# A four-layer graph network: inverse roots on another engine, and every engine's instructions in the order of the program

## The chip, the core and the metric

The kernel runs on one core of one Trainium2 chip. A core has TensorE (PE in the profile: matrix products, with the weight loads shown apart as PEld), VectorE (DVE), ScalarE (ACT: functions from tables, which a table load switches), GpSimd (POOL), and SyncE (SP), which issues the DMA transfers here. Each engine has its own list of instructions, fixed when the program is built, and takes them one after the other; an instruction that needs another engine's result waits on a semaphore, and all behind it in that list wait with it. The metric is the device time of one execution in microseconds.

## The reference

64 graphs of 256 nodes with 128 features and an adjacency of zeros and ones (`x` is 64x256x128, `adj` 64x256x256, float32) go through four layers. After each layer the input is added and the sum normalised over the features:

- layer 0: `max_j relu(p_i + q_j + b) * adj_ij`, with `p = x (W1 - W2)` and `q = x W2`
- layer 1: `tanh([adj @ elu(x Win), elu(x Wnode), adjT @ elu(x Wout)] Wupd)`
- layer 2: two graph convolutions with `dinv_i (adj + I)_ij dinv_j`, where `dinv = 1/sqrt(degree)`, with elu between
- layer 3: for each edge `gelu(layernorm(m_j + m_i + b))` (128 features), summed over the neighbours; then a linear update with a layer normalisation of its own.

```
def _layernorm(x, axis=-1, eps=1e-5):
    m = jnp.mean(x, axis=axis, keepdims=True)
    v = jnp.var(x, axis=axis, keepdims=True)
    return (x - m) / jnp.sqrt(v + eps)
...
msg = jax.nn.gelu(_layernorm(pre, g1, be1), approximate=False)
agg = jnp.einsum('bijo,bij->bio', msg, adjacency)
```

## The kernel before

About one in eight entries of `adj` is set, so layers 0 and 3 work on edges, not on all pairs. For each graph the nodes are sorted by their number of neighbours, and the k-th neighbours of all nodes stand side by side in slot k of a row of 4800 columns for each half of the nodes. A one-hot matrix `hot` (fp8) picks the neighbour of each column. A product of `hot` with the features, which are split into three bf16 parts so that no precision is lost, fetches them: three matmuls for each 512 columns. If a graph didn't fit the slots, a flag would start a second way (`general`); with these inputs it is not run.

Each graph goes through four generators, in this order:

- `first` (L502 to L711): `nz` and `diff` from `adj` (L509, L511), the transposed adjacency `aT` (L516, L519), counts by matmul, the rank of each node by four ACT sign instructions (L551), the permutation `perm` (L560), the slots (`nzp`, `rank`, `lack`, L566 to L592), 24 DVE instructions that make `hot` (L629; the last slots L635), `q` split into three parts (L647 to L652), and ten tiles for each half: PE fetches 512 columns into one of four PSUM banks `bigp` (L665, and L681, which lowers empty slots), DVE takes the maximum into `lanes` (L492 in `fold`). Then come the way back through the permutation (L691 to L706), `y` (L709), and a layer normalisation.
- `second` (L215): layer 1, small products and elus (ACT exp, L194).
- `third` (L261 and L789 on): layer 2, the factors of layer 3 (L797 to L815), and the sums for the first four of the ten tiles of 1024 or 704 columns.
- `last` (L821): the rest of layer 3. For a tile, `sums_of` has PE fetch (L728), DVE add the node's own part (L732), ACT square (L736), PE sum the squares (L743) and ACT write a row (L745) that goes to DRAM; for two tiles together the row comes back as 16 columns (`vr`), is turned into `1/sqrt` (L768) and goes out again (L771); each tile's scale is spread to all partitions by a DMA (`rs_s`, L828). Then DVE multiplies (L839), ACT takes the gelu (L841), DVE adds up (L492, `sums`), and PE applies the output weights (L860) and the permutation (L870).

`inverse_root` (L72) is a Sqrt on ACT and a reciprocal on DVE. It is used by the layer normalisation on two columns (`rs`), for `dinv` on two, and for `vr` on 16.

`together` (L341) runs the four generators of four consecutive graphs next to each other: round u has `last` of graph u, `third` of u+1, `second` of u+2, `first` of u+3, and each is advanced by one `yield` at a time, in proportion to the weights in `STAGES` (L879). That is the order in which the program is written down. The order on each engine is another one: the recording layer has a scheduler that plans with its own estimate of durations, and places each instruction where it may start by that plan, so work of one round can pass work of the round before. Four PSUM banks `mm` (L357) go round among all stages for the small products. The load of `x` and `adj` stands at the start of `first`.

## Time and profile before

| what | us |
|---|---|
| time of the runs: median, lowest, highest of three | 5728.43, 5723.99, 5739.29 |
| the profiled execution: its own time | 5731.62 |
| its span in the profile | 5729.7 |
| PE busy (79% of the span) | 4529.9 |
| PEld busy (44%) | 2508.7 |
| DVE busy (84%) | 4834.4 |
| ACT busy (75%) | 4275.2 |
| POOL busy | 1.9 |
| mean granted TensorE clock, as a share of full speed | 0.862 |

A group's row in the profile has the line, the engine, the operation, output and input with their shapes and the number of instructions; behind the first bar their busy time and the mean length of one in ns; behind the second the idle time of the engine just before them, with what ended most of it. The chain of waits is followed back from the last instruction: at each step to what released it, or to the instruction before it on its engine. In the timeline a row has its start, its length, the engine and line, and what it is.

### The profile page before, as it was taken

To read this page: it belongs to the slowest core of one execution; us is meant where nothing else is said; L and a number is where in the kernel's file an instruction comes from. 1 tells how busy PE (TensorE), PEld (TensorE's weight loads), DVE (VectorE), ACT (ScalarE), POOL (GpSimd) and SP (SyncE) were. 2 spreads that over 40 slices of the span, in tenths; PEclk is the share of its full clock that TensorE was granted. 3 is DMA by queue.
4 is the path that set the end of the run, shared out by engine and by line. 5 is a ranking of instruction groups with operands and counts; after the bars stand their busy time and mean duration, and the time that the engine had idled before them with its cause. 6 is when DMAs were issued, how large, how long until landed. Compare 5 with 4: busy or idle time off the path is not lost.

```text
span 5729.7 us, 83531 instructions
## 1 busy us (share of the span) xinstructions
PE 4529.9 (79%) x27408; PEld 2508.7 (44%) x27408; DVE 4834.4 (84%) x14654; ACT 4275.2 (75%) x6485; POOL 1.9 (0%) x10
## 2 busy tenths in 40 slices
PE   5878878878778778788788788787887887877875
PEld 2444444444444444444444444444444444444443
DVE  6788888888888888888888888888888888888876
ACT  2577777777777777777777777777777777777785
POOL 0000000000000000000000000000000000000000
PEclk8888889889889889888898898898888887888986
DMA  0122222222212221221221222122212212221222
GB/s 22 44 70 63 62 63 72 62 63 66 69 57 70 65 63 63 72 63 62 63 72 62 63 65 70 59 68 65 63 62 72 64 62 63 69 66 60 68 65 74
DMA packets 292813, 365.15 MB, mean 64 GB/s; under 512 B 151952, under 2 KB 210448, under 8 KB 292368
## 3 DMA queue, kind: packets, MB, share of 16 engines
q1 hardware_dynamic: 292368, 359.73, 20.0%
q8 instruction: 217, 3.56, 0.3%
q14 instruction: 228, 1.87, 0.1%
HBM read 345.07 MB, written 14.53 MB: 63 GB/s over the span
## 4 chain that ended last, share of the span: by engine, by line
PE 52%; DVE 29%; ACT 11%; issue 4%; DMA 3%; SPq 0%; DVEq 0%; POOL 0%; ACTq 0%
PE bigp L665 11%; PE bigp L728 8%; DVE pre L839 6%; PE mm L860 5%; DVE lanes L492 4%; PE mm L743 4%; DVE hot L629 4%; DVE pre L732 4%; DVE sums L492 3%; PE bigp L681 3%; DMA rs_s<-scale_line 2%; PE mm L870 2%; PE mm L296 2%; PE mm L699 2%; PE mm L647 2%
## 5 line engine op out<-in xcount | busy, mean ns | idle before, releaser
L665 PE MATMUL bigp<-hot,q 128*128 128x512 fp8e4 (+1 forms) x3840 | 1052.3, 371 | 66.6 <-DVE lanes L492 52.6
L728 PE MATMUL bigp<-hot,c 128*128 128x512 fp8e4 (+1 forms) x3840 | 928.8, 372 | 140.2 <-DVE pre L732 140.2
L732 DVE TENSOR_TENSOR pre<-bigp,dT 128x512 f32<-128x512 f32 (+6 forms) x1664 | 846.3, 530 | 37.8 <-PE bigp L728 33.5
L492 DVE TENSOR_TENSOR lanes<-bigp,lanes 128x512 f32<-128x512 f32 (+6 forms) x1536 | 772.7, 503 | 94.6 <-PE bigp L681 86.9
L839 DVE TENSOR_TENSOR pre<-pre,rs_s 128x1024 f32<-128x1024 f32 (+1 forms) x640 | 732.9, 1150 | 48.6 <-DMA rs_s<-scale_line 48.0
L736 ACT ACTIVATE sq<-pre 128x1024 f32<-128x1024 f32 (+1 forms) x640 | 638.5, 998 | 169.9 <-DVE pre L732 163.9
L841 ACT ACT_TABLE_LOAD x535 | 686.4, 1283 | 9.5
L492 DVE TENSOR_TENSOR sums<-pre,sums 128x1024 f32<-128x1024 f32 (+6 forms) x1024 | 628.8, 614 | 41.2 <-ACT pre L841 40.7
L745 ACT ACTIVATE row<-mm,eps_t 128x256 f32<-128x256 f32 (+1 forms) x640 | 289.6, 453 | 476.9 <-PE mm L743 476.7
L841 ACT ACTIVATE pre<-pre,be,g 128x1024 f32<-128x1024 f32 (+1 forms) x512 | 594.2, 1172 | 57.8 <-DVE pre L839 53.0
L743 PE MATMUL mm<-sq,ones 128*32 128x256 f32 (+1 forms) x5120 | 482.9, 440 | 135.2 <-ACT sq L736 135.2
L74 ACT ACT_TABLE_LOAD x445 | 570.9, 1283 | 7.5
L728 PEld LDWEIGHTS <-c 128*128 128x128 bf16 x3840 | 331.2, 98 | 550.5 <-issue 136.1
L665 PEld LDWEIGHTS <-q 128*128 128x128 bf16 x3840 | 310.8, 97 | 392.6 <-issue 112.0
L296 PE MATMUL mm<-aT,hs 128*128 128x256 f32 x512 | 232.3, 600 | 316.1 <-DVE hs L293 214.8
L629 DVE TENSOR_SCALAR hot<-rank 128x512 fp8e4<-128x512 bf16 (+5 forms) x1536 | 440.5, 348 | 0.0
L681 PEld LDWEIGHTS <-pick 42*128 42x128 bf16 x2944 | 155.8, 95 | 481.5 <-issue 474.2
L296 PEld LDWEIGHTS mm<-aT,hs 128*128 128x128 f32 x512 | 135.6, 293 | 425.8 <-issue 316.1
L860 PE MATMUL mm<-w3u,sums 128*128 128x128 f32 x2048 | 296.7, 289 | 18.4 <-DVE sums L492 16.1
L194 ACT ACT_TABLE_LOAD x221 | 283.5, 1283 | 3.9
L681 PE MATMUL bigp<-lack,pick 42*128 42x36 bf16 (+16 forms) x2944 | 285.7, 187 | 0.0
L860 PEld LDWEIGHTS mm<-w3u,sums 128*128 128x128 f32 x2048 | 254.5, 195 | 37.3 <-issue 17.6
(226 smaller groups left out, 7132.6 us busy)
## 6 DMA issues: line engine op xcount, KB each, us to landing
rs_s<-scale_line SPq DMA_DIRECT2D x512, 512.0 KB
rs_s<-scale_line SPq DMA_DIRECT2D x128, 352.0 KB
an<-in_adj SPq DMA_DIRECT2D x64, 256.0 KB
x<-in_x SPq DMA_DIRECT2D x64, 128.0 KB
line<-row SPq DMA_DIRECT2D x512, 4.0 KB
out<-o SPq DMA_DIRECT2D x64, 128.0 KB
fu<-fulls SPq DMA_DIRECT2D x192, 4.0 KB
vr<-line SPq DMA_DIRECT2D x192, 8.0 KB
```

The lines of the kernel that those rows point to most:

```text
L74: nc.scalar.activation(t, t, AF.Sqrt)
L492: nc.vector.tensor_tensor(lanes[:, :k, :w], src[:, i:i + k], lanes[:, :k, :w], op)
L629: nc.vector.tensor_scalar(hot[:, :, at:at + w], rank[:, :, :w], s0 + i + 1.0 - FAR, None, ALU.is_equal, saturate=False)
L665: nc.tensor.matmul(pt[:, :tl], q3[:, i, h], hot[:, h, t0:t0 + tl], start=i == 0, stop=False)
L681: nc.tensor.matmul(o_, l_, r_, start=False, stop=i == len(todo) - 1)
L728: nc.tensor.matmul(pt[:, :bl], c3[:, k, h], hot[:, h, t0 + b:t0 + b + bl], start=k == 0, stop=k == 2)
L732: nc.vector.tensor_add(block(pre[:, b:], n, w, at), block(pt, n, w, at), widen(dT[:, h, :w], n))
L736: nc.scalar.activation(sq[:, :tl], pre[:, :tl], AF.Square)
L743: nc.tensor.matmul(pr[q * Q:(q + 1) * Q, :tl // 4], ones[:, :Q], v4[:, :, q], start=True, stop=True)
L839: nc.vector.tensor_mul(pre[:, :tl], pre[:, :tl], rs[:, :tl])
L841: nc.scalar.activation(msg[:, :tl], pre[:, :tl], AF.Gelu, bias=be3, scale=g3)
L860: nc.tensor.matmul(pt[:, cols], lanes[:, k, cols], w3u[:, 1], start=k == 0, stop=False)
```

## The change

- `inverse_root` becomes one GpSimd instruction, the power with exponent -0.5 (a tile `mhalf`). The two products that follow it, for `vr` and `dinv`, go to GpSimd as well.
- The whole edge-wise path is recorded with `tc.manual_schedule` for all five engines: each takes its instructions in the order in which the program writes them.
- The generators are cut into more steps: a `yield` stands wherever the work passes from one engine to another, so that steps of other graphs come between. The weights in `STAGES` are new.
- Each stage has one PSUM bank `mm` of its own (tags `_f`, `_s`, `_t`, `_l`) in place of four shared by all, and small tiles of its own. The four `bigp` banks stay.
- `dinv` is worked out in `first`; in layer 2, `aT` is scaled by it once (two DVE instructions of 128x256) in place of `hs` twice (four of 128x128).
- `x` and `adj` of a graph are loaded at the end of `first` of the graph before. The transposes of `perm` move beside the making of `hot`. Each fetch of `first` stands one tile ahead of the maximum.
- Layer 3 runs five tiles ahead (was four), with `pre` in eight buffers (was seven); `row` has one buffer (was two), `rs_s` two (was three). The way of `vr` through DRAM is a generator of its own (`scales`), advanced by one step with each step of its stage. The scale of a tile is fetched one tile ahead (was two).

```diff
-    half = consts.tile([P, N], F32, name="half")
-    nc.vector.memset(half, 0.5)
+    mhalf = consts.tile([P, 16], F32, name="mhalf")
+    nc.vector.memset(mhalf, -0.5)
     def inverse_root(t):
-        nc.scalar.activation(t, t, AF.Sqrt)
-        nc.vector.reciprocal(t, t)
+        nc.gpsimd.tensor_tensor(t, t, mhalf[:t.shape[0], :t.free_size()], ALU.pow)
...
             nc.vector.tensor_scalar(rs, mv[:, :, 1], EPS, None, ALU.add)
-            yield
             inverse_root(rs)
+            yield
             yield
...
             if twice:
                 nc.vector.tensor_scalar(e, e, 1.0, None, ALU.min)
+                yield
                 nc.scalar.activation(e, e, AF.Exp, bias=minus1)
...
+        def inverse_root_of(self, deg, bufs):
+            nc.vector.tensor_scalar(deg, deg, 1.0, None, ALU.add)
+            pos = self.work.tile([P, H], F32, name="pos" + self.tag)
+            nc.vector.tensor_scalar(pos, deg, 0.0, None, ALU.is_gt)
+            dinv = self.state.tile([P, H], F32, name="dinv", bufs=bufs)
+            nc.vector.tensor_scalar(dinv, deg, 1e-30, None, ALU.max)
+            inverse_root(dinv)
+            nc.gpsimd.tensor_mul(dinv, dinv, pos)
+            return dinv
...
+            for h in range(H):
+                nc.vector.tensor_scalar(aT[:, h], aT[:, h], dinv[:, h:h + 1], None, ALU.mult)
...
             for step in (1, 2):
-                for h in range(H):
-                    nc.vector.tensor_scalar(hs[:, h], hs[:, h], dinv[:, h:h + 1], None, ALU.mult)
...
-        ps_mm = ctx.enter_context(tc.tile_pool(name="ps_mm", bufs=4, space=bass.MemoryType.PSUM))
+        ps_mm = ctx.enter_context(tc.tile_pool(name="ps_mm", bufs=1, space=bass.MemoryType.PSUM))
...
-        sh = Shared(work, state, ps_mm)
-        psum = sh.psum
+        sh_f, sh_s, sh_t, sh_l = (Shared(work, state, ps_mm, tag) for tag in ("_f", "_s", "_t", "_l"))
...
+        def loads(g, s):
+            s["x0"] = xn = sh_f.node_tile("x0")
+            nc.sync.dma_start(xn, x[ds(g, 1)].rearrange("b (h p) d -> p (b h) d", p=P))
+            s["an"] = an = state.tile([P, H, N], F32, name="an")
+            nc.sync.dma_start(an, adj[ds(g, 1)].rearrange("b (h p) j -> p (b h) j", p=P))
...
+            nc.vector.tensor_scalar(dg, dg, 1.0 / N, None, ALU.mult)
+            s["dinv"] = sh_f.inverse_root_of(dg, 4)
+            yield
...
                         sign, pd[:, h * N:(h + 1) * N], AF.Sign, bias=kc[:, hi, h:h + 1], accum_out=more[:, h, hi:hi + 1]
                     )
             yield
+            yield
...
+            pts = {0: fetch_tile(*banks[0])}
+            yield
...
+            for k, (h, t0, tl) in enumerate(banks):
+                if k + 1 < len(banks):
+                    pts[k + 1] = fetch_tile(*banks[k + 1])
+                pt = pts.pop(k)
+                next(rest, None)
+                if t0 == 0:
+                    lanes = work.tile([P, 2, N], F32, name="lanes")
+                    nc.scalar.copy(lanes, pt.rearrange("p (s k) -> p s k", s=2))
+                else:
+                    fold(lanes, pt, t0, tl, ALU.max)
+                if t0 + tl == WIDTH:
+                    rest = largest(h, lanes)
+                    next(rest)
+                yield
...
+            if "next" in s:
+                loads(*s["next"])
+            s["x1"] = sh_f.node_tile("x1")
+            yield from sh_f.layernorm(s["x1"], y)
...
-        AHEAD = 4
+        AHEAD = 5
...
+        def scales(s, i, line):
+            yield
...
+            nc.sync.dma_start(vr[:rows], line[:, :n].rearrange("o (p k) -> (o p) k", k=PIECE))
...
+            yield
             inverse_root(vr[:rows])
-            nc.vector.tensor_mul(vr[:rows], vr[:rows], fu[:rows])
+            nc.gpsimd.tensor_mul(vr[:rows], vr[:rows], fu[:rows])
+            yield
...
+        def with_chains(s, gen):
+            for _ in gen:
+                for c in list(s["chains"]):
+                    if next(c, s) is s:
+                        s["chains"].remove(c)
+                yield
...
             for i in range(len(TODO) + 1):
+                square_sums(s, i + AHEAD - 1, psum)
+                gather_tile(s, i + AHEAD)
                 if i < len(TODO):
+                    spread_scales(s, i + 1)
...
                     nc.vector.tensor_mul(pre[:, :tl], pre[:, :tl], rs[:, :tl])
                     msgs[i] = msg = pre if t0 else big.tile([P, TILE], F32, name="sums")
                     nc.scalar.activation(msg[:, :tl], pre[:, :tl], AF.Gelu, bias=be3, scale=g3)
                     yield
+                if i + AHEAD - 1 < len(TODO):
+                    squares_out(s, i + AHEAD - 1)
+                    add_own(s, i + AHEAD)
+                    yield
...
-        STAGES = [(last, 34), (third, 34), (second, 14), (first, 44)]
+        IN_ORDER = ("PE", "Activation", "DVE", "Pool", "SP")
+        STAGES = [(last, 35), (third, 42), (second, 18), (first, 58)]
...
+        with tc.manual_schedule(engines={mybir.EngineType[e] for e in IN_ORDER}):
+            if U == B:
+                steps(0)
```

`sums_of` is cut into `gather_tile` (PE), `add_own` (DVE, then the square on ACT), `square_sums` (PE) and `squares_out` (ACT and the DMA); `spread_scales` is the DMA of `rs_s`.

## The prediction

> **What bounds the kernel now.** I read the busy totals first, then the busy times of one round, then the start times of one graph's `first`, and the groups of instructions and the waits last.
>
> ```profile
> PE 4529.9 (79%) x27408; PEld 2508.7 (44%) x27408; DVE 4834.4 (84%) x14654; ACT 4275.2 (75%) x6485; POOL 1.9 (0%) x10
> ...
> PE 52%; DVE 29%; ACT 11%; issue 4%; DMA 3%; SPq 0%; DVEq 0%; POOL 0%; ACTq 0%
> ...
> L841 ACT ACT_TABLE_LOAD x535 | 686.4, 1283 | 9.5
> ...
> L74 ACT ACT_TABLE_LOAD x445 | 570.9, 1283 | 7.5
> ...
> L194 ACT ACT_TABLE_LOAD x221 | 283.5, 1283 | 3.9
> ```
>
> No engine is full, and the chain of waits changes engine all the time. 1236 table loads (x 1.283 = 1586 us) are over a third of ACT's time. Next, one round from the view of busy times by stretch (length; PE, weight loads, DVE, ACT and POOL busy; PE's granted clock; DMA share; GB/s), and then from the view by source line when a line's first and last instruction in some rounds start.
>
> ```profile
> 2007.40:2094.70 87.30, 71.40 (x440) 39.54 (x439) 74.86 (x229) 66.51 (x104) 0.00 (x0) 0.90 0.20 65
> ```
>
> ```profile
> L509 DVE TENSOR_SCALAR nz<-an x3: 422/422/423, 2008.2 to 2182.4; 128x512 bf16<-128x512 f32 x3
> ...
> L665 PE MATMUL bigp<-hot,q x60: 246/379/634, 2071.9 to 2115.3; 128*128 128x512 fp8e4 x54, 128*128 128x192 fp8e4 x6
> ...
> L709 DVE SCALAR_TENSOR_TENSOR y<-m,x x2: 415/417/419, 2036.8 to 2123.9; 128x256 f32<-128x256 f32 x2
> ```
>
> `nz`, the first step of `first`, comes every 87.1 us (2008.2, 2182.4 two rounds later). PE is busy for 71.4 of that, DVE for 74.9, ACT for 66.5. The graph whose `nz` is at 2008.2 fetches its tiles (L665) from 2071.9 to 2115.3, and has its `y` (L709) at 2123.9: its `first` takes 116 us, 29 us more than a round. It fits because the `nz` of the next graph is at 2096.2, 28 us before that `y`. This overlap of two `first` stages is what I look at most.
>
> **Prices.** They are the rows by shape; the timeline shows that neighbours on one engine overlap (the add at 2094.57 lasts 0.69 and the next begins after 0.60), so in sums I take start to next start, and the full length where another engine waits.
>
> ```profile
> L839 DVE TENSOR_TENSOR pre<-pre,rs_s 128x1024 f32<-128x1024 f32 x512 | 622.3, 1216 | 22.8 <-DMA rs_s<-scale_line 22.2
> ...
> L736 ACT ACTIVATE sq<-pre 128x1024 f32<-128x1024 f32 x512 | 538.7, 1052 | 167.2 <-DVE pre L732 163.9 <-DVE total_m L688 3.1 <-DVE hs L308 0.2
> ...
> L841 ACT ACTIVATE pre<-pre,be,g 128x1024 f32<-128x1024 f32 x384 | 476.6, 1241 | 55.8 <-DVE pre L839 51.8
> ...
> L551 ACT ACTIVATE sign<-mm,kc 128x256 bf16<-128x256 f32 x256 | 121.1, 473 | 5.6 <-DVE dg L544 2.5 <-DVE kc L542 1.9
> ```
>
> ```profile
> 2094.57 0.69 DVE L732 TENSOR_TENSOR pre<-bigp,dT 128x512 f32<-128x512 f32 x1
> 2095.17 0.68 DVE L492 TENSOR_TENSOR lanes<-bigp,lanes 128x512 f32<-128x512 f32 x1
> ...
> 2038.85 1.28 ACT L74 ACT_TABLE_LOAD   x1
> 2040.14 0.20 ACT L74 ACTIVATE rs<-rs 128x2 f32<-128x2 f32 x1
> ```
>
> **The root on POOL.** Gone from ACT: 576 square roots (64.4 + 40.5 + 27.6 + 13.0 = 145 us) and, with the new order, 731 table loads: the built order has 505 where there were 1236. At 1.283 us, with no gap before the next instruction (2038.85 + 1.28, then 2040.14), that is 938 us; ACT falls to some 3190 us, 50 us a round. From DVE go the reciprocals (137 us), two small products (59 us) and L293 (61 us); scaling `aT` adds 128 at about 0.3 (39 us). Added up from start to start, 73.3 us a round are left of 75.2. Neither saving shortens a round unless ACT or DVE ended it.
> [...]
> POOL gets 17 instructions a round (1088 in all). The trace has no such power. From below I take its shortest row, 0.10 us; from above its longest, 0.45 (the select of 42x192), although a power may exceed it: its powers have 2 columns (six) or 16 (five), nearest to the small rows. A power takes the place of a load, a root and a reciprocal (1.28 + 0.20 + 0.15), and most have a step of cover on DVE: I take 0. At 2 us each, two or three would stand bare at the ends of `layernorm`, +5 us a round.
> [...]
>
> **The order.** Now all of `first` of a graph comes before all of `first` of the next in every engine's list: the 28 us of overlap are gone, and a round can't be shorter than one `first` with everything that the lists put between its steps. I added up the lists of one full round, with 0 at the start of `nz`.
> *To the split of q.* Before it DVE has 36.2 us: five multiplies L839 5.4, adds L732 5.9, sums L492 4.8, one-hot L629 and L635 7.0, the rest 13.1. At six places it has nothing left that it may do:
> - `kc`: the `aT` copy stands behind a square, which stands behind adds ending at 3.4; square to 4.5, copy 4.8, transpose 5.1, copy 5.5, counts 5.9. DVE is at 4.5: 1.4 us.
> - adds: their gather (PE square sums 0.70, three matmuls 0.69) follows the counts, so 7.3 instead of 6.7: 0.6. They end at 8.7.
> - `place`: that square to 9.8, four signs at 0.56 to 12.1, or 12.4 if the matmuls of `pd` (10.0) come late; DVE is done at 9.4: 3.0.
> - the first elu: load and exp (1.28 + 0.42) end at 14.1, DVE at 13.6: 0.5.
> - the second: the multiply ends at 16.3, then ACT has gelu 1.24, a copy 0.5, a load 1.28 and the exp 0.5, to 19.8. DVE has adds of 1.2: 2.4.
> - `lack_t`: the multiply ends at 22.8; load to 23.5, gelu to 24.7, `lack` 0.69, to 25.4: 2.6.
>
> Together 10.5, so the split is done at 46.7.
> *The fetch.* PE's list has the 2.6 us of L860 in front; 1.1 of it are late. From the first fetch to the end of the last it has 35.4 us (sixty L665 and their L681: 17.9; L728 4.1, L743 1.4, L860 2.6, L870 and L325 2.6, the layers' matmuls the rest). DVE's 25.8 beside it are hidden. PE can't be ahead: the four `bigp` banks and q hold it.
> *The tail.* DVE's remaining 11.3, with 1.8 of waits (0.6 for the last gather, 0.8 for `m0` behind sixteen L699, the rest for `mk`): 13.1. `x` and `adj` of the next graph are fetched in its cover: at the start of the trace `an` took 3.0 us from issue (32.6) to `nz` (35.6), and SP reaches the issue before the last 5 us. SP stops at each DMA that waits for ACT or POOL, but what stands behind it (`rs_s`) is used 8 us later: 0, at most 3.0 a round if `an` is late.
>
> Round: 46.7 + 1.1 + 35.4 + 13.1 = 96.3 us, against 87.2.
> **The sum.** There are 61 full rounds; 5729.7 - 61 x 87.2 = 410 us are the preparation and six partial rounds, which I leave, since less overlap there stands against less ACT work. 410 + 61 x 96.3 = 6284; the waits I could not see (semaphores, DMA) add a little: 6290. The profiled run took 5731.6 us, 1.9 more than its span and 3.2 more than the median of 5728.4, so nothing is corrected.
>
> **Rivals.** The round that changes nothing is 87.2, so 4.3 us of waits at the joints on top of 36.2 + 35.4 + 11.3 = 82.9 decide.
> 1. *The joints close* (faster): ACT's 938 us less were what held DVE, and the lists run without the waits above: 410 + 61 x 82.9 = 5467, up to 5711. For it: ACT is full (4.3 of 4.4 us) in most slices between `sign` and `hot` of the round shown, half with loads. Against it: the three largest waits (8.0) hold from row lengths alone. It decides where all waits are below 4.3 us.
> 2. *Half of the waits*: of the 13.4 us of waits (10.5 + 1.1 + 1.8) half stay: 82.9 + 6.7 = 89.6, 5876 us. For it: some of my PE prices are those of a low clock (L296 0.43 from start to start, where L238 of the same shape takes 0.23).
> [...]
> 4. The root doesn't leave ACT: the built order has no Sqrt, so I give it nothing.
>
> **Chances.** My forecast, 6080 to 6560 (rounds of 93 to 100.8): 0.57. Rival 2, 5780 to 6080 and down to +0.3%: 0.14. Rival 3, above 6560: 0.05. Within 0.3%, about what a measurement of this kernel can tell from no change: 0.03. Rival 1: 0.21. So slower 0.76, same 0.03, faster 0.21. The range from 5640 to 6560 holds the first two, the same and a quarter of rival 1: 0.79. The forecast's own range is 6080 to 6560.
>
> **What would show it.** Right: table loads 505; ACT below 3300 us; `nz` to `nz` near 96 with the next `nz` *after* `y`; DVE busy near 4690 us but 75% of the span; waits of DVE for `sign`, `lack` and the elu's exp of 2 to 3 us, 64 times each. Wrong: rounds below 87 with PE and DVE both above 80%; or POOL rows above 1 us with DVE waiting for `rs`. I am wrong if DVE reaches those places later than my sums say, so that ACT is ready.

## The result and the profile after

The changed kernel takes 6895.3 us (median; 6893.2 to 6895.3) where the kernel before takes 5728.4: **1.203 times as long, 95% interval 1.200 to 1.206**. The forecast of 6290 us had the direction and less than half of the loss; the time lies outside its range of 5640 to 6560.

The profiled execution took 6893.2 us with a span of 6891.4. Busy times, and one group of table loads, from its page:

```profile
PE 4900.1 (71%) x27408; PEld 2668.3 (39%) x27408; DVE 5027.4 (73%) x13438; ACT 3228.2 (47%) x5050; POOL 1570.9 (23%) x1098
...
L954 ACT ACT_TABLE_LOAD x252 | 323.3, 1283 | 4.4
```

ACT fell by 1047 us, as its loads did (1236 to 505). PE and DVE have the same or less to do and are *longer* busy: by 370 and 193 us. A round, from the view of busy times by stretch, and the steps of one `first`, from the view by source line:

```profile
3078.70:3184.50 105.80, 75.94 (x428) 41.46 (x428) 77.90 (x209) 50.63 (x79) 24.54 (x18) 0.82 0.18 53
```

```profile
L523 DVE TENSOR_SCALAR nz<-an x2: 417/418/419, 3078.7 to 3184.7; 128x512 bf16<-128x512 f32 x2
...
L698 PE MATMUL bigp<-hot,q x60: 246/379/634, 3130.8 to 3167.0; 128*128 128x512 fp8e4 x54, 128*128 128x192 fp8e4 x6
...
L765 DVE SCALAR_TENSOR_TENSOR y_f<-m,x x1: 426/426/426, 3180.6 to 3180.6; 128x256 f32<-128x256 f32 x1
```

A round is 105.8 us (before 87.2, forecast 96.3), and the next `nz` comes 4.1 us after `y`: the two `first` no longer overlap. The fetch starts 52.1 us after `nz`, takes 36.2 from its first start to its last, and 17.7 are left behind that. Two rows of the timeline stand ahead of the fetch, the end of the split of `q` (3127.77, 49.1 us after `nz`) and L938 (L860 before), ahead of which PE stood for 4.80 us:

```profile
3127.34 0.43 DVE L510 TENSOR_TENSOR q<-rest,q 128x256 bf16<-128x256 f32 x1
3126.12 2.04 PE L938 MATMUL mm_l<-w3u,sums 128*128 128x128 f32 x8 [4.80 <-DVE sums L501]
```

The groups of DVE and ACT that the sum was made with have kept their lengths:

```profile
L952 DVE TENSOR_TENSOR pre<-pre,rs_s 128x1024 f32<-128x1024 f32 x512 | 623.0, 1217 | 36.9 <-DMA rs_s<-scale_line 36.9
L803 ACT ACTIVATE sq<-pre 128x1024 f32<-128x1024 f32 x512 | 540.2, 1055 | 1136.1 <-DVE pre L799 1122.9 <-DVE y_s L272 4.4 <-DVE z L184 3.7
L954 ACT ACTIVATE pre<-pre,be,g 128x1024 f32<-128x1024 f32 x384 | 477.7, 1244 | 615.7 <-DVE pre L952 614.9
...
L569 ACT ACTIVATE sign<-mm_f,kc 128x256 bf16<-128x256 f32 x256 | 120.1, 469 | 12.7 <-PE mm_f L562 6.4
```

The waits (engine and tile that waited, what for; us in total, how often, the longest):

```profile
DVE lanes L501 <- PE bigp L714: 661.9, 458, 4.6
DVE place L575 <- ACT sign L569: 194.2, 64, 3.3
DVE m L762 <- ACT m L760: 162.0, 64, 5.0
DVE lack_t L618 <- ACT lack L604: 157.8, 64, 4.2
DVE elu_e_t L201 <- ACT elu_e_t L199: 150.8, 64, 2.4
DVE kc L552 <- PE mm_f L546: 93.0, 64, 2.2
```

Divided by 64: `place` 3.03 us, `lack_t` 2.47, the second elu 2.36, `kc` 1.45. The forecast had 3.0, 2.6, 2.4 and 1.4. But two rows are not as forecast: `m` (2.53 a round; 0.8 was taken) and DVE's wait for the fetch (662 us; 86.9 before). The rest of the document looks for the 9.5 us a round that were not foreseen.

### The profile page after: what moved, and what is told of

Read it like the earlier page. It is cut to its first block, busy times and chain, and to the rows that moved or that the text cites. A ratio compares the mean times of both kernels' runs of the same rounds, so it can differ in the third digit from the quotient of the medians.

```text
span 6891.4 us, 81950 instructions
## 1 busy us (share of the span) xinstructions
PE 4900.1 (71%) x27408; PEld 2668.3 (39%) x27408; DVE 5027.4 (73%) x13438; ACT 3228.2 (47%) x5050; POOL 1570.9 (23%) x1098
## 5 line engine op out<-in xcount | busy, mean ns | idle before, releaser
L75 POOL TENSOR_TENSOR vr<-vr,mhalf 128x16 f32<-128x16 f32 (+1 forms) x320 | 1195.6, 3736 | 1606.8 <-DMA vr<-line 1603.3
L698 PE MATMUL bigp<-hot,q 128*128 128x512 fp8e4 (+1 forms) x3840 | 1078.9, 392 | 7.2 <-ACT q L505 6.4
L786 PE MATMUL bigp<-hot,c 128*128 128x512 fp8e4 (+1 forms) x3840 | 1010.7, 406 | 0.0
L952 DVE TENSOR_TENSOR pre<-pre,rs_s 128x1024 f32<-128x1024 f32 (+1 forms) x640 | 735.9, 1150 | 37.6 <-DMA rs_s<-scale_line 37.6
L501 DVE TENSOR_TENSOR sums<-pre,sums 128x1024 f32<-128x1024 f32 (+6 forms) x1024 | 637.2, 622 | 17.7
L938 PE MATMUL mm_l<-w3u,sums 128*128 128x128 f32 x2048 | 406.6, 361 | 323.6 <-DVE sums L501 323.6
L75 POOL TENSOR_TENSOR rs_s<-rs_s,mhalf 128x2 f32<-128x2 f32 x64 | 44.5, 696 | 2237.3 <-DVE rs_s L174 2237.3
L938 PEld LDWEIGHTS mm_l<-w3u,sums 128*128 128x128 f32 x2048 | 358.2, 260 | 376.3 <-issue 347.0
L661 DVE TENSOR_SCALAR hot<-rank 128x512 fp8e4<-128x512 bf16 (+5 forms) x1536 | 458.6, 352 | 0.0
L698 PEld LDWEIGHTS <-q 128*128 128x128 bf16 x3840 | 323.1, 102 | 268.3 <-issue 45.3
L954 ACT ACTIVATE sums<-pre,be,g 128x1024 f32<-128x1024 f32 x128 | 158.7, 1240 | 496.0 <-DVE pre L952 496.0
L305 PE MATMUL mm_t<-aT,hs 128*128 128x256 f32 x512 | 253.5, 650 | 139.0 <-DVE hs L202 139.0
L814 PE MATMUL mm_l<-sq,ones 128*32 128x256 f32 (+1 forms) x3072 | 305.7, 481 | 32.1 <-ACT sq L803 32.1
L305 PEld LDWEIGHTS mm_t<-aT,hs 128*128 128x128 f32 x512 | 151.7, 326 | 451.6 <-DVE hs L202 428.8
L814 PE MATMUL mm_t<-sq,ones 128*32 128x256 f32 x2048 | 189.7, 447 | 162.9 <-ACT sq L803 162.9
```

Source lines behind the costliest of these rows:

```text
L75: nc.gpsimd.tensor_tensor(t, t, mhalf[:t.shape[0], :t.free_size()], ALU.pow)
L305: nc.tensor.matmul(pa[:, :N], hs[:, h], aT[:, h], start=h == 0, stop=h == H - 1)
L501: nc.vector.tensor_tensor(lanes[:, :k, :w], src[:, i:i + k], lanes[:, :k, :w], op)
L661: nc.vector.tensor_scalar(hot[:, :, at:at + w], rank[:, :, :w], s0 + i + 1.0 - FAR, None, ALU.is_equal, saturate=False)
L698: nc.tensor.matmul(pt[:, :tl], q3[:, i, h], hot[:, h, t0:t0 + tl], start=i == 0, stop=False)
L786: nc.tensor.matmul(pt[:, :bl], s["c3"][:, k, h], s["hot"][:, h, t0 + b:t0 + b + bl], start=k == 0, stop=k == 2)
```

## The experiments

Times are medians, ratios stand against the kernel before on the same chip, and "round" is `nz` to `nz` in the steady part of the trace (before 87.2, changed 105.8).

**The root by itself, the order by itself.** First the root alone is undone in the changed kernel.

```diff
-        nc.gpsimd.tensor_tensor(t, t, mhalf[:t.shape[0], :t.free_size()], ALU.pow)
+        nc.scalar.activation(t, t, AF.Sqrt)
+        nc.vector.reciprocal(t, t)
```

> The changed kernel with the root alone put back (Sqrt on ACT, reciprocal on DVE); lists, steps and PSUM banks as in the changed kernel. Theory 'order' (the slowdown comes from lists that follow the program): the root's place matters little to the end. A layernorm then ends on a load, a root and a reciprocal (1.28 + 0.20 + 0.15 = 1.63 us) where the power takes 0.70; the 16-column powers of 4 us become about 1.8 us, but most of these lie beside DVE work; up to 730 more loads come at joints where ACT is waited for: 6850 to 7250 us, never near 5728. Theory 'POOL' (the powers of 0.7 and 4 us, and POOL beside DVE, make the loss): a round loses most of its 19 us more, so 5730 to 6300 us, and L501, L799 and L952 become shorter or wait less.

Measured: 7667.9 us, ratio 1.340 [1.338, 1.342], 1212 table loads, a round of 117.9. In ordered lists the root on POOL does not cost, it saves 773 us, more than the expectation allowed: DVE waits 788.8 us for the root of `vr` alone.

Then the order alone is undone, everything else as changed.

```diff
-        with tc.manual_schedule(engines={mybir.EngineType[e] for e in IN_ORDER}):
-            if U == B:
...
+        if U == B:
```

> The changed kernel's program, buffers, banks and POOL root, but the engines' lists are made by the planner as before instead of following the program. Theory 'order': most of the loss goes, 5500 to 5900 us; nz of the next graph lies before y again or DVE's start-to-start times fall back (L501 at 0.62, L171 at 0.45). Theory 'banks': if a PSUM bank and single buffers for each stage forbid the overlap whatever the order, it stays above 6300 us with DVE and PE waiting for each other at the shared tiles. Theory 'POOL': above 6300 us with waits for the powers.

Measured: 5943.2 us, 1.040 [1.038, 1.043], 43 above what the theory of the order expected. **The fixed lists cost 952 us of the loss of 1167; what is left, 215 us, is the program.** Where those are, three kernels tell. Two are the kernel before, planned, with the power in place of the root: everywhere, and only for two columns.

```diff
-        nc.scalar.activation(t, t, AF.Sqrt)
-        nc.vector.reciprocal(t, t)
+        nc.gpsimd.tensor_tensor(t, t, mhalf[:t.shape[0], :t.free_size()], ALU.pow)
```

> The kernel before with the root alone moved to POOL; the planner orders the engines and 'first' of two graphs overlaps as before. Theory 'order': ACT loses some 700 loads and 576 roots (about 1000 us of 4370), POOL is waited for at few places because two graphs give the planner other work: 5450 to 5740 us, nz to nz 83 to 87.3 us. Theory 'POOL': powers of 0.7 and 4 us stand bare at the ends of the normalisations, or DVE becomes longer row by row: 5950 us or more. If ACT's loads were no bound at all, within 0.5% of 5728.

```diff
+        if t.free_size() == 2:
+            nc.gpsimd.tensor_tensor(t, t, mhalf[:t.shape[0]], ALU.pow)
+            return
         nc.scalar.activation(t, t, AF.Sqrt)
```

> The kernel before, planned, with the power on POOL only where the root has two columns (rs, dinv; 384 of them at 0.70 us by the run with all of them); the 16-column roots stay on ACT. Theory 'long powers' (the loss of 272 us in the run with all powers is DVE standing 752 us before the product with fu for powers of 2.9 us and more): that wait is gone, and ACT still loses some 390 roots and their loads: 5600 to 5740 us. Rival 'any power' (0.70 us bare at each end of a normalisation, or a planner that orders worse when ACT is lighter): 5800 to 6000 us.

Measured: 5997.8 us with all powers, 1.049 [1.047, 1.050], and 5688.9 us with the short ones, 0.994 [0.992, 0.996]. With all powers ACT is busy for 3096 us instead of 4275, with 379 table loads, and no gain is seen. The short powers alone make ACT 404 us lighter (954 loads), and the time falls by 0.6%. So ACT's load hardly bounded the kernel before. What the long powers cost is this wait, of DVE with the product that follows the power on `vr`:

```profile
DVE vr L770 <- POOL vr L76: 752.2, 319, 5.1
```

The third is the changed program, planned, with the 16-column roots back on ACT and DVE.

```diff
-        nc.gpsimd.tensor_tensor(t, t, mhalf[:t.shape[0], :t.free_size()], ALU.pow)
+        if t.free_size() == 2:
+            nc.gpsimd.tensor_tensor(t, t, mhalf[:t.shape[0], :2], ALU.pow)
+            return
+        nc.scalar.activation(t, t, AF.Sqrt)
+        nc.vector.reciprocal(t, t)
...
-        with tc.manual_schedule(engines={mybir.EngineType[e] for e in IN_ORDER}):
```

> The changed kernel's program, banks and single buffers, planned, with the 16-column roots back on ACT and DVE; the two-column ones stay on POOL. Theory 'long powers' (they alone cost the planned changed kernel its 220 us, as they cost the kernel before 309 us between all powers and short powers): 5600 to 5740 us. Rival 'banks' (a bank and buffers for each stage take freedom from the planner): 5800 us or more.

Measured: 5751.3 us, 1.005 [1.003, 1.006], 11 above the range for the long powers. 192 of the 215 us go with them; they lie on the way of the scale: DVE waited 565.5 us for `rs_s` with them, and 42.4 without. While the order is planned, a PSUM bank and buffers for each stage cost next to nothing (23 us are left); in fixed lists no run tells their price.

**Is it the lost overlap?** The forecast put the loss on the 28 us by which two `first` overlapped. In the kernel before, planned, an instruction was put behind `y` that reads `nz`, so that the only `nz` tile stays taken; first one that reads `nz` alone, then one that reads `y` too.

```diff
             nc.vector.scalar_tensor_tensor(y, m0, 0.0, xn, ALU.max, ALU.add)
+            held = work.tile([P, 1], BF16, name="held")
+            nc.vector.tensor_tensor(held, nz[:, 0, :1], y[:, 0, :1], ALU.max)
```

> The kernel before, planned as before, but nz is held until y: a DVE copy of one column of nz after y (128 elements, about 0.1 us) keeps the only nz tile, so nz of the next graph can't come before y. Leaves nothing else out. Theory 'order, by the overlap': the 28 us of overlap are gone while the planner still interleaves the other stages, so a round is one 'first' plus the turn from y to nz. 'first' was 116 us when it shared the engines with the next one; alone it may shrink. Theory expects nz to nz of 95 to 112 us, 6200 to 7250 us in all. Rival 'the overlap is worth little, the list itself (dependent neighbours, waits at the head) is what costs': nz to nz stays under 91 us, under 5960 us.

> The kernel before, planned, and nz held until y by a DVE instruction of one column that reads nz and y (the only nz tile can't be written again before it; in the run before this one the copy read nz alone, and the planner put it 10 us after nz, so it held nothing). Theory 'overlap' (the two 'first' stages beside each other are what the ordered lists lose): the next nz comes after y, a round becomes one 'first' of 95 to 116 us, 6200 to 7490 us. Rival 'lists' (the planner makes up for the overlap with the other stages; what costs in the changed kernel is the fixed order within a stage): a round stays under 91 us, 5700 to 5960 us.

The first was placed 18 us behind `nz` (not 10, as the second expectation says), far ahead of `y`, so it held nothing and changed nothing (5726.7 us, 1.0005 [0.9995, 1.0015]). The second did what it should, and **the time fell**: 5679.5 us, 0.993 [0.991, 0.994]. By source line, four rounds of it:

```profile
L509 DVE TENSOR_SCALAR nz<-an x4: 391/396/399, 2019.4 to 2278.6; 128x512 bf16<-128x512 f32 x4
...
L709 DVE SCALAR_TENSOR_TENSOR y<-m,x x4: 418/420/421, 2017.9 to 2277.1; 128x256 f32<-128x256 f32 x4
```

Each `nz` now comes 1.5 us after a `y`, and three rounds take 259.2 us, 86.4 each; a `first` alone takes 84.9 us instead of 115.4 on average. The overlap was slack that the planner had and did not need. The theory of the lost overlap falls, and with it the sentence that the forecast looked at most.

**Whose list is it?** The changed kernel with DVE's list alone planned, and with those of PE and ACT planned.

```diff
-        IN_ORDER = ("PE", "Activation", "DVE", "Pool", "SP")
+        IN_ORDER = ("PE", "Activation", "Pool", "SP")
```

> The changed kernel with DVE's list alone made by the planner; PE, ACT, POOL and SP keep the program's order. Theory 'DVE's list' (dependent neighbours on DVE, +322 us from start to start and 132 us of short gaps, and DVE standing at the head of its list for sign, lack, m and the elus, 760 us): DVE takes other work there and a good half of 1150 us comes back: 5750 to 6350 us, L501 and L171 at their old start-to-start times. Rival 'graph order' (PE's and ACT's lists alone forbid the overlap, and each engine's fixed list makes the others wait): 6600 to 7000 us.

```diff
-        IN_ORDER = ("PE", "Activation", "DVE", "Pool", "SP")
+        IN_ORDER = ("DVE", "Pool", "SP")
```

> The changed kernel with the lists of PE and ACT made by the planner; DVE, POOL and SP keep the program's order. With DVE's list alone planned 622 us of the 952 between the ordered and the planned changed kernel came back. Theory 'DVE's list' (it alone sets the round: it stands still in its places and its dependent neighbours cost): less than 150 us come back, 6750 to 6910 us. Rival 'shares add up' (PE's and ACT's fixed lists own the other third by themselves): 952 - 622 = 330 us come back, 6480 to 6650 us.

Measured: 6272.9 us (1.096 [1.094, 1.098], round 95.6) and 6247.1 us (1.092 [1.090, 1.094], round 95.3). Each gives back about two thirds of the 952 us, 622 and 648; for the second, one theory expected less than 150 and the other 330. The shares don't add up: no one list owns the loss. That it comes where two fixed lists meet, so that freeing either side of the meeting place gives most of it back, is argued from this, not shown place by place.

**Is it the length of the powers?** A POOL product by 0.001 in their place, which leaves the inverse roots out.

```diff
-    nc.vector.memset(mhalf, -0.5)
+    nc.vector.memset(mhalf, 1e-3)
...
-        nc.gpsimd.tensor_tensor(t, t, mhalf[:t.shape[0], :t.free_size()], ALU.pow)
+        nc.gpsimd.tensor_tensor(t, t, mhalf[:t.shape[0], :t.free_size()], ALU.mult)
```

> The changed kernel with a POOL product by 0.001 in place of each power (leaves the inverse roots out; the same tiles, lists and waits, rows of some 0.2 us instead of 0.70 and 2.9 to 4.1). The difference to the changed kernel is the price of the power's length in an ordered list. Theory 'order': six short powers of which up to five are bare, 0.5 us each, and the long ones in the cover of DVE's work: 2.5 us a round at most 4, 6640 to 6860 us. Theory 'POOL': the powers stand on the chain at every normalisation and sums line: 10 us a round or more, below 6300 us.

Measured: 6888.8 us, ratio 1.204 [1.202, 1.206], 7 us less. The rows of POOL in the changed kernel, and then in this one:

```profile
L75 POOL TENSOR_TENSOR vr<-vr,mhalf 128x16 f32<-128x16 f32 x192 | 779.7, 4061 | 1174.5 <-DMA vr<-line 1174.5
...
L75 POOL TENSOR_TENSOR rs_l<-rs_l,mhalf 128x2 f32<-128x2 f32 x128 | 89.1, 696 | 223.5 <-DVE rs_l L174 223.5
```

```profile
L75 POOL TENSOR_TENSOR vr<-vr,mhalf 128x16 f32<-128x16 f32 x192 | 277.6, 1446 | 1341.0 <-DMA vr<-line 1340.6 <-issue 0.2
...
L75 POOL TENSOR_TENSOR rs_l<-rs_l,mhalf 128x2 f32<-128x2 f32 x128 | 25.0, 195 | 453.4 <-DVE rs_l L174 453.4
```

2.6 us less for each long row and 0.5 for each short one, and almost nothing is won, less than either theory expected. No step of the round comes earlier: the fetch starts 52.3 us after `nz` and `y` 102.2 (52.0 and 101.8 with the powers). In these ordered lists the powers' length is covered, or nearly: by DVE's own waits it stood bare for 22.7 us (`rs_f`). A few tenths of a microsecond a round could be hidden here, since both rounds are 105.8 us for the reason found under "Whole windows".

**What lies next to what on DVE.** The planned kernel puts other work between instructions that feed each other; the program's order does not. From the timeline, the statistics of a normalisation before, and then after:

```profile
2036.84 0.42 DVE L709 SCALAR_TENSOR_TENSOR y<-m,x 128x256 f32<-128x256 f32 x1
2037.17 0.34 DVE L180 TENSOR_SCALAR o<-z,mv,rs 128x128 f32<-128x128 f32 x1
2037.43 0.48 DVE L171 BATCH_NORM_STATS2 st<-y 128x6 f32<-128x128 f32 x2
2037.82 0.17 DVE L172 BATCH_NORM_AGGREGATE mv<-st 128x2 f32<-128x6 f32 x1
```

```profile
3180.61 0.43 DVE L765 SCALAR_TENSOR_TENSOR y_f<-m,x 128x256 f32<-128x256 f32 x1
3181.07 0.29 DVE L171 BATCH_NORM_STATS2 st_f<-y_f 128x6 f32<-128x128 f32 x1
3181.40 0.18 DVE L172 BATCH_NORM_AGGREGATE mv_f<-st_f 128x2 f32<-128x6 f32 x1
3181.50 0.26 DVE L171 BATCH_NORM_STATS2 st_f<-y_f 128x6 f32<-128x128 f32 x1
3181.80 0.18 DVE L172 BATCH_NORM_AGGREGATE mv_f<-st_f 128x2 f32<-128x6 f32 x1
3182.01 0.17 DVE L174 TENSOR_SCALAR rs_f<-mv_f 128x2 f32<-128x2 f32 x1
```

Before, `o` begins 0.09 us before `y` ends. After, a `bn_aggr` begins 0.04 *behind* the end of the `bn_stats` that it reads. Over the whole trace of the changed kernel, a neighbour (at most 50 ns behind) that by its tiles' names reads or overwrites the tile just written begins 22 ns before its forerunner's end on average, another one 83 ns before it; and there are 7449 of the first kind to 4745 of the second (before: 4101 to 9223). The 22 ns is a mean of two values: 3612 of the 7449 begin 83 ns before the end as strangers do, many on another part of the same tile, and 3837 begin behind it, by 34 ns in the median (before: 457). Such a pair costs 117 ns more than two strangers. One experiment moves two such pairs in each normalisation apart.

```diff
             for h in range(H):
                 nc.vector.bn_stats(st[:, h], src[:, h])
+            for h in range(H):
                 nc.vector.bn_aggr(mv[:, h], st[:, h])
```

> The changed kernel, ordered, with one thing moved: in a normalisation the two bn_stats come first and then the two bn_aggr, so that no bn_aggr directly follows the bn_stats that it reads. Theory 'dependent neighbours' (in this kernel's DVE list a neighbour that reads its forerunner's output begins 22 ns before its end, another 83 ns): two joints of each of the five normalisations win about 0.06 us, 0.6 us a round, 40 us: 6840 to 6865 us. Rival 'they don't matter, DVE waits elsewhere anyway': within 0.2% of the changed kernel, 6881 to 6909 us.

Measured: 6692.1 us, 1.169 [1.167, 1.171]: 203 us less, five times the expectation. In its trace the statistics take 0.74 us from the first `bn_stats` to `rs`, where the rows above take 0.94:

```profile
3090.51 0.49 DVE L171 BATCH_NORM_STATS2 st_f<-y_f 128x6 f32<-128x128 f32 x2
3090.91 0.30 DVE L173 BATCH_NORM_AGGREGATE mv_f<-st_f 128x2 f32<-128x6 f32 x2
3091.25 0.17 DVE L175 TENSOR_SCALAR rs_f<-mv_f 128x2 f32<-128x2 f32 x1
```

Five times 0.20 is 1.0 us a round, 61 us; the round fell by 3.4, and the fetch starts no earlier (52.0 us after `nz`). Another thing must have moved.

**TensorE at half clock.** In the changed kernel's trace the clock that is granted to PE is 1.00 or 0.50, in 323 stretches of each, and each stretch but the last, which the end of the trace cuts off, takes a whole number of windows of 3.413 us (81 take one). PE's rows give it away. By shape, before, and then after:

```profile
L860 PE MATMUL mm<-w3u,sums 128*128 128x128 f32 x2048 | 296.7, 289 | 18.4 <-DVE sums L492 16.1
...
L699 PE MATMUL mm<-mk,permT 128*128 128x128 f32 x1024 | 127.7, 279 | 0.0
```

```profile
L938 PE MATMUL mm_l<-w3u,sums 128*128 128x128 f32 x2048 | 406.6, 361 | 323.6 <-DVE sums L501 323.6
...
L754 PE MATMUL mm_f<-mk,permT 128*128 128x128 f32 x1024 | 217.2, 401 | 0.9 <-ACT mk L729 0.9
```

These are the same matmuls under new line numbers. From one start to the next, L938 takes 112 ns at a clock of 1.00 and 213 at 0.50 in the median, and so does L754. And by stretch, one window of the clock, and then the two places in one round of the changed kernel, ahead of the fetch and ahead of `m` (the third number from the end is the granted clock):

```profile
3120.77:3124.18 3.41, 0.56 (x3) 0.15 (x1) 3.24 (x14) 2.90 (x4) 0.10 (x1) 1.00 0.46 150
3126.10:3130.80 4.70, 4.68 (x21) 3.86 (x22) 3.21 (x8) 1.29 (x2) 2.89 (x1) 0.50 0.38 114
3175.90:3179.30 3.40, 3.40 (x22) 3.28 (x24) 1.34 (x6) 0.80 (x2) 0.00 (x0) 0.57 0.66 222
```

PE stood 4.80 us before the first place (its wait for `sums`) and 1.30 and 1.97 us, with little work between, before the second. Added up over the trace, 1071 us of PE's busy time lay in half-clock stretches before, 1772 after; half of the 701 more is 350, close to the growth of PE's busy time (370). In the experiment above, L754's row falls from 401 to 315 ns though nothing of PE's list was touched. Its time in half-clock stretches falls from 3.0 to 0.9 us a round, and that of the fetch (L698) from 2.9 to 0.3; half of the difference is 2.3 us, which with the 1.0 of the pairs makes up the 3.4 (an estimate). The drops and rises go with PE's busy time in the window ahead: in the first row PE is busy for 0.56 of 3.41 us, and the clock drops at its end. At the median of the trace's 323 drops it was busy for a quarter of the window ahead (0.59 of it at the most), and ahead of a rise for 0.79 of it at the least.

To test it, PE was given work that nobody reads in its idle places: first in the tail.

```diff
+            def fill(pt, n):
+                for _ in range(n):
+                    nc.tensor.matmul(pt, q3[:, 0, 0], hot[:, 0, 0:512], start=True, stop=True)
...
                 pt = psum()
+                if h == H - 1:
+                    fill(pt, 7)
                 for hk in range(H):
...
+            fill(ps_big.tile([P, 512], F32, name="bigp"), 8)
             yield
             pm = psum()
```

> The changed kernel, ordered, with 15 matmuls more a round in the tail, whose results nobody reads: 7 of 128x512 before the second transpose of total_m (PE stands 1.30 us there) and 8 after it (1.97 us). They give PE work in a stretch after which the trace has it at half the granted clock, so that the sixteen matmuls of L754 take 0.21 us each instead of 0.11. Theory 'half clock' (the changed kernel's larger idle places put PE at half clock on the path, and the round sits on a whole number of clock windows of 3.413 us, 31 now): L754 at 0.11 wins 1.7 us although PE has 3.3 us more work, and the round falls to 102.40 (30 windows), 6680 to 6700 us, or, if it doesn't sit on whole windows, to 104.1, 6780 to 6800 us. Rival 'DVE and ACT set the tail': within 0.2% of 6891 us, or the extra matmuls come on top: 6950 to 7100 us.

Measured: 6712.2 us, 1.173 [1.171, 1.175]: **with 960 more matmuls the kernel is 183 us faster**, and L754 is at 277 ns. The round is 102.7 on average. In about half of the trace rounds of 101.7 and 103.1 us alternate, two of them together 204.8 us or 60.0 windows; elsewhere they are longer. The expectation's lower time was missed by 12 us.

Then with the pairs apart, and 22 more between `q` (L681) and L938.

```diff
+                    nc.tensor.matmul(pt, ident_b, hot[:, 0, 0:512], start=True, stop=True)
+
+            fill(ps_big.tile([P, 512], F32, name="bigp"), 22)
             q3 = work.tile([P, 3, H, P], BF16, name="q3")
```

> The changed kernel, ordered, with the statistics pulled apart, the 15 matmuls in the tail, and 22 more (128x512, read by nobody) between q (L681) and the eighteen L938 ahead of the fetch, where PE stands some 5 us and then runs L938 and the first fetches at half clock (4.2 us of L938 and 2.9 us of L698 in each round; 0.3 and 0 in the kernel before). Theory 'half clock': L938 at 0.11 to 0.2 and L698 at 0.22 win 2 to 3 us before and at the start of the fetch, on top of about 1 us for the pairs and 1.7 us for the tail: a round of 98 to 100 us (29 windows are 98.99), 6390 to 6510 us. Rival 'DVE sets the start of the fetch' (the split of q3 ends no earlier): what the two edits win at most, 102 us, 6640 to 6700 us.

Measured: 6513.5 us, 1.137 [1.135, 1.139], a round of 99.3. The two kinds of rows, and the clock at the two places:

```profile
L947 PE MATMUL mm_l<-w3u,sums 128*128 128x128 f32 x2048 | 292.6, 287 | 35.5 <-DVE sums L502 35.5
...
L763 PE MATMUL mm_f<-mk,permT 128*128 128x128 f32 x1024 | 126.4, 277 | 0.0
```

```profile
3149.20:3153.50 4.30, 4.30 (x29) 2.87 (x27) 4.09 (x13) 2.13 (x4) 1.03 (x2) 1.00 0.08 15
3194.40:3196.60 2.20, 2.20 (x21) 1.71 (x18) 2.13 (x11) 0.49 (x2) 0.87 (x2) 1.00 0.09 13
```

Against the changed kernel the fetch starts 1.8 us earlier in the round, is 1.5 shorter, and the tail 3.1: 6.4 of the 9.5 us. The burst of L938 ahead of the fetch takes 2.5 us instead of 4.6. L938, the fetch and L754 lie in half-clock stretches for 0.3 us a round instead of 10.0; half of the difference is 4.9 us, and about 1.0 is DVE's pairs by the reading above (estimates). Against the kernel with the pairs apart, the added matmuls alone make 179 us. The gain is a little short of what the theory of the clock expected (6513.5 us for 6390 to 6510).

**Whole windows.** In the changed kernel a round is 31.0 windows of 3.413 us; with the product 31.0, with the statistics apart 30.0. In the second and third of these the rounds differ, from the seventh on, by a standard deviation of 0.03 and 0.06 us. It is no rule of ordered lists: with DVE planned the mean is 28.0, but the rounds vary by 0.51 us, and with the root back on ACT, all lists in order, a round is 34.6 windows and varies by 0.71. The planned kernels have 25.3 to 26.8 and vary by 0.66 us and more. If a round holds on to a whole number, small gains and losses don't show. Additions that nobody reads were put on DVE's path in the kernel with the statistics apart, three, six and twelve.

```diff
+            late = work.tile([P, P], BF16, name="late")
+            for _ in range(3):
+                nc.vector.tensor_add(late, y[:, 0], own[:, 0])
```

> The ordered kernel with the statistics pulled apart (6692 us, round 102.40 us = 30.00 windows) and, after y of 'first', three DVE additions of 128x128 that nobody reads, some 0.2 us each from start to start: 0.6 to 0.75 us more on DVE's path in each round. Theory 'whole windows' (the round holds on to a whole number of 3.413 us clock windows; a small delay only moves it against the windows): round 102.40, 6680 to 6705 us; or, if the step lies right here, 105.81 and 6885 to 6910 us. Rival 'linear': 61 rounds of 0.6 to 0.75 us more, 6729 to 6738 us.

> The same with six such additions, 1.2 to 1.5 us more in each round. Theory 'whole windows': 6680 to 6705 us or 6885 to 6910 us and nothing between. Rival 'linear': 6765 to 6784 us.

> The same with twelve such additions, 2.4 to 3.0 us more in each round. Theory 'whole windows': 105.81, 6885 to 6910 us. Rival 'linear': 6838 to 6875 us.

An addition took 0.326 us from start to start, not 0.2, so the delays are 0.98, 1.96 and 3.91 us. Measured: 6756.7, 6906.2 and 6912.6 us (1.180 [1.178, 1.182], 1.207 [1.205, 1.208], 1.208 [1.206, 1.210]). `nz` in a stretch of the last two (six of them, five rounds):

```profile
L524 DVE TENSOR_SCALAR nz<-an x6: 416/417/419, 3085.3 to 3614.3; 128x512 bf16<-128x512 f32 x6
```

```profile
L524 DVE TENSOR_SCALAR nz<-an x6: 416/418/422, 3097.7 to 3626.8; 128x512 bf16<-128x512 f32 x6
```

Both give 105.8 us a round, 31.0 windows, with delays that differ by 1.95. From 102.4, the delay of 1.96 cost 3.41 us and that of 3.91 cost 3.42. With the measured delays the linear rival would give 6812 and 6931 us; six additions cost more than that, and twelve cost less. The delay of 0.98 cost 0.96 a round on average, as the linear rival has it (6692 + 61 x 0.98 = 6752 us), and the time lies in neither range of the theory. But these rounds go from 102.7 to 104.6, and in about half of the trace four in a row make 413.0 us, 121.0 windows. So there are plateaus at whole numbers, and between them a mean that moved with the delay. That the shift of the late bursts of PE against the windows makes the plateaus is argued from this, not shown step by step.

**Small gains in planned kernels.** Both edits that made the kernel before faster, together (the diffs of the short powers and of the held `nz`); and the held `nz` in the changed program, planned, with short powers.

> The kernel before, planned, with both edits that made it faster by themselves: nz held until y (by 47 us) and the two-column roots on POOL (by 37 us). If they act at different places: 5620 to 5660 us. If both only relieve the same joint: 5670 to 5700 us.

> The changed kernel's program, planned, with the 16-column roots back on ACT (5751 us without the next edit) and nz held until y. Theory 'the held nz helps the planner' (47 us won in the kernel before): 5690 to 5720 us. Rival 'edits of this kind move a planned kernel by about 1% in either direction, as their sum did (5785 us, where each alone was at 5679 and 5689)': anywhere from 5690 to 5810 us, and no gain can be put down to the edit.

Measured: 5785.3 us, 1.010 [1.008, 1.011], and 5830.6 us, 1.017 [1.015, 1.019]. Both times lie outside all the ranges expected, the second by 21 us from the widest. The sum of two gains is a loss, and the same edit wins 47 us in one program and loses 79 in another. A planner that places everything anew moved by up to 1.7% here (5688.9 to 5785.3). The two fastest kernels (0.993 and 0.994) are faster than the kernel before and the changed one, but neither gain can be put down to its edit.

## Why the prediction was right and wrong

The direction was right, the account only in part. The first term that failed is the 46.7 us to the split of `q`, and the largest misses are matmuls priced at full clock, ahead of the fetch and in the tail.

- **The root on POOL, "I take 0".** Right for this kernel, as far as a round that holds on to whole windows can show it: with the powers' length gone the time is the same within 7 us, and DVE's wait for `rs_f` is 22.7 us in all. The bounds failed: a power took 0.70 us for two columns and 3.2 to 4.1 for 16, where 0.10 to 0.45 stood, with "may exceed it" beside. In a planned kernel the long ones cost 192 to 309 us. DVE's rows did not grow beside POOL: L952 has kept its length (1216 ns before, 1217 after). That ACT's savings shorten a round only if ACT or DVE ended it fits the runs: 857 fewer loads in the kernel before, with all powers, showed no gain.
- **"73.3 us a round left" on DVE** was right for a planned order (the changed program, planned, has 4704 us, where near 4690 was forecast) and wrong for the ordered one (77.9 a round, 5027 us). The step took "start to next start" from a trace in which 553 DVE instructions begin up to 50 ns behind the end of the one ahead; in the ordered one 3844 do, nearly all of them on the tile just written, in the planned form of the same program 338. At 83 ns of lost overlap, the 3506 more are 291 of the 323 us between these two forms (an estimate).
- **The order, "this overlap is what I look at most".** Wrong: with the overlap forbidden and the planner left, a round is 86.4 us. What made a round longer were the fixed lists.
- **"To the split of q", 46.7.** This is the step that failed first: it ends at 49.1. The waits for `place`, `lack_t`, the elu and `kc` are each within 0.2 us of the forecast; that of the adds for their gather is 1.5 where 0.6 stood. All six make 11.1 instead of 10.5, and DVE's own work, from start to start and with its short gaps, 37.9 instead of 36.2. Here 21 neighbours a round begin behind the end of the one ahead; at 117 ns each they are 2.5 us (an estimate), enough for the 1.7.
- **"The fetch", 1.1 us late and then 35.4.** The fetch begins at 52.0 after `nz`, not at 47.8, and its first to last start take 36.0. Of the 4.2 us, 2.2 are DVE's: L938 can start at 47.4, where the sum had it at 45.2 (2.6 us ahead of the fetch). The other 2.0 are its price: 4.6 us to the first fetch instead of 2.6, and 2.5 with PE kept busy. L860 and the fetch were priced by rows of a trace that has them at full clock (0.2 of L860's 4.6 us a round in half-clock stretches, 0.2 of the fetch's 16.4). After, it is 4.2 of 6.4 and 2.9 of 16.9. A wait of DVE or ACT had been counted as idle time of PE that costs nothing; PE's next burst ran at half speed (L938 213 ns from start to start where 112 do).
- **"The tail", 13.1.** 17.8 measured, in the main for the same reason: "0.8 for `m0` behind sixteen L699" became 2.53. With PE kept busy it is 0.97, and the tail 14.7.
- **The sum.** 410 + 61 x 105.8 = 6864 against a span of 6891: the frame held. Of 4.2 + 0.6 + 4.7 = 9.5 us a round missing, 6.4 were given back by keeping PE at full clock and parting the pairs. Of the other 3.1, 2.3 lie before the end of the split, which stays at 49.1; the rest is not told apart.
- **The rivals.** The joints didn't close, nor half of them. Rival 3, for which POOL's powers are slow (2 us each, +5 us a round), came nearest in time, with a chance of 0.05 and a cause that the runs contradict: without the powers' length the kernel is 7 us faster. None of them names the clock on the path, though the reason given for rival 2, "some of my PE prices are those of a low clock", had its row in hand and looked only at prices that could fall.

## What to carry to other kernels

Before costing a new order, ask of each engine's price in which order it was measured: in these runs a row's start-to-start time on DVE belonged to its neighbours (83 ns of overlap, or a gap of 34), and a matmul's to the idle time ahead of it (L754's row 401 ns, and 277 with work in the idle places). A wait that was moved onto PE was paid twice here, once as idle time (4.80 us ahead of L938) and once as half clock behind it (4.6 us of L938, and 2.5 with PE kept busy), and filling it with matmuls that nobody reads was the cheaper of the two (183 us won in the tail). In a kernel with a fixed, repeating order, judge a small edit by more than one size of it: here a round held on to 31.0 clock windows with delays of 1.96 and 3.91 us alike, and an edit worth 1.0 us (an estimate) took 3.4 off it.

## What the runs showed of the hardware that was not expected

- In the changed kernel's trace a power on POOL takes 0.70 us at the least for 128x2 and 2.89 for 128x16; a product 0.19 (`dinv`) and 0.22 (`vr`).
- In the same trace a DVE instruction begins 83 ns before the end of the one ahead in the median; of the 7449 that read or overwrite the tile just written, 3837 begin behind that end, by 34 ns in the median.
- POOL's rows grew beside DVE, not the reverse. In the changed kernel L952 on 128x1024 takes 1219 ns on average in the 71 cases in which it begins while POOL is at work, and 1216 in the other 441. The power on 128x16 takes 2.89 to 3.77 us in the 131 cases with no L661 beside it, and 5.15 to 6.96 in the 61 with one; in 58 of these the power began before the first L661. The product of `vr` on 108x16 takes 0.25 us on average, and 1.19 in the program's planned form. What makes the rows grow, no run shows.
- PE at half clock on the path cost more than 960 matmuls that nobody reads (183 us less with them), and rounds of some ordered kernels came out as whole numbers of 3.413 us windows (31.0 and 30.0).
